# A pair-update kernel whose input is also laid out channel-major by the host, so that its first stage transposes no x

## The chip, the cores and the metric

One core of one Trainium2 chip runs the whole program. The metric is device time in microseconds (us) for one execution, lower is better; the kernel before is the median of three runs.

## The reference

x is 1 x 384 x 384 x 128 (i, j, channel), all float32. Two layers follow each other; cut to what is computed:

```python
# layer 0
z     = layernorm(x) * g + b
left  = (z @ Wl + bl) * sigmoid(z @ Wlg + blg)
right = (z @ Wr + br) * sigmoid(z @ Wrg + brg)
core  = einsum('bikh,bjkh->bijh', left, right)
zo    = (layernorm(core) * og + ob) @ Wout + bout
x1    = x + sigmoid(x @ Wg + bg) * zo
# layer 1
left  = x1 @ W_left + b_left + x1 @ W_eq + b_eq
right_sum = sum over j of (x1 @ W_right + b_right)
out   = (left * right_sum * sigmoid(x1 @ W_gate + b_gate)) @ W_out + b_out
y     = layernorm(out + x1) * scale + bias
```

## The kernel before

The program has three stages, one after the other; only their ends overlap.

**Stage 1** (source lines 100 to 403) makes `left` and `right`. A token is one (i, k) pair of x. The 384 x 384 tokens are cut into 144 chunks of 8 rows i by 128 tokens k, numbered so that 8 chunks (64 rows i of one block of 128 k) form a group; there are 18 groups. A chunk is two steps of 4 rows, so there are 288 steps and 16 steps in a group. `steps` (L352) lists them, and the loop at L368 writes out by hand what each engine is given in each step; `seq` keeps that order on every engine and DMA queue.

What happens to a step: `load_chunk` (L113) brings tokens on partitions and channels along the free axis. `stats` (L234) runs `bn_stats` and `bn_aggr` on VectorE (DVE), for the step that lies `AHEAD` = 6 steps further on. `powers` (L246), on GpSimd (POOL), makes for each token `rs` = 1/std and `nd` = mean - std, eight rows at a time, once per chunk. `shift` (L262), on GpSimd, subtracts `nd` from the 4 x 128 values of each token, two steps ahead. `front` (L272) transposes the four 128 x 128 blocks on TensorE (PE) and copies the result from PSUM on ScalarE (ACT), so that channels lie on partitions (`zt`). `back` (L319), called twice a step for two rows each, multiplies two blocks of `zt` by the folded 128 x 512 weights `wz`; ScalarE takes the sigmoid of the gate half with `rs` as its scale, and VectorE multiplies (L339) into a tile `lr` of one group (8 MiB, two buffers). The constant part of the layer norm is folded into `wz` with the matrix `avg` (`fold`, `weights`).

What stage 1 stores: `store_zt` (L299) writes each shifted and transposed step to the scratch tensor `xt_d`; `store_nd` (L301) transposes the `nd` of one group (64 rows) and writes it to `nd_d`; `store_slice` (L313) writes a finished group from `lr` to `lr_d`, one slice of 1 MiB per step, in the first eight steps of the next group. The last two groups stay in SBUF. All these DMAs are issued by SyncE (SP) in one order, and a DMA that waits holds up those behind it.

**Stage 2** (to L551) does, for each of 128 channels h, nine accumulating 128x128 by 128x384 matmuls (L516), and writes `core_d` and sums for the second layer norm. In its shade `early_x` (L484) rebuilds x for the first `TR` = 16 rows: it reads `nd` as a broadcast over partitions, adds `xt_d` by an accumulating DMA issued from GpSimd, and stores `xf_d`.

**Stage 3** runs over the 384 rows i: `front` (L633) makes the gate from x, `scale_core`, `layer0`, `gated_left`, `layer1`, the row layer norm, and `store`. Its x comes channel-major through `load_x` (a broadcast of `nd_d`, four rows at a time) and `add_x` (L588; an accumulating DMA from GpSimd that adds `xt_d`).

The four instructions of `powers`, which the prediction counts:

```python
seq(nc.gpsimd.tensor_scalar(sd, mv[:, :, 1], EPS, 1.0, ALU.add, ALU.mult))
seq(nc.gpsimd.tensor_tensor(rs, sd, mhalf[:, :hi - lo], ALU.pow))
seq(nc.gpsimd.tensor_tensor(sd, sd, rs, ALU.mult))
seq(nc.gpsimd.tensor_tensor(nd, mv[:, :, 0], sd, ALU.subtract))
```

Of the kernel before, what the change touches and what calls it, by code (L numbers as in the profile page):

```python
# [19 lines left out]
def triangle_then_gated_row_kernel(ctx: ExitStack, tc: tile.TileContext, a: dict, out: bass.AP):  # L20
# [14 lines left out]
    x = a["x"].rearrange("b i j c -> (b i) j c")  # L35
    y = out.rearrange("b i j c -> (b i) j c")
    N, _, C = x.shape
# [9 lines left out]
    TR = 16  # L47
# [6 lines left out]
    xt_d = dpool.tile([C, N, NB, P], F32, name="xt_d")  # L54
    nd_d = dpool.tile([N, N], F32, name="nd_d")
    xf_d = dpool.tile([C, TR, N], F32, name="xf_d")

# [24 lines left out]
    with ExitStack() as ctx2:  # L82
# [17 lines left out]
        with tc.tile_pool(name="p1w", bufs=6, side="right") as wp, \  # L100
             tc.tile_pool(name="p1x", bufs=6, side="right") as xp, \
             tc.tile_pool(name="p1s", bufs=5, side="right") as sp, \
             tc.tile_pool(name="p1z", bufs=6, side="right") as ztp, \
# [4 lines left out]
            AHEAD = NQ + 4  # L108
            HS = H // 8
            loaded, normed = {}, {}  # L110
            lr, full = {}, []

            def load_chunk(n, part=slice(0, XR)):  # L113
                if n < len(chunks):
                    kb, ig, c = chunks[n]
                    i0 = ig * G + c * XR
                    if part.start == 0:
                        loaded[n] = xp.tile([P, XR, C], F32, tag="xt", name="xt")
                    src = x[i0:i0 + XR, kb * P:(kb + 1) * P, :].rearrange("i k c -> k i c")
                    seq(nc.sync.dma_start(out=loaded[n][:, part], in_=src[:, part]))  # L120


            load_chunk(0, slice(0, 4))

            stage = lrp.tile([P, H, G, 2], F32, tag="lr", name="stage").rearrange("p h i s -> p (h i s)")

# [7 lines left out]
            seq(nc.vector.memset(avg, 1.0 / P))  # L136
# [21 lines left out]
            def fold():  # L158

                busy(2)
                busy(1, 1)
                seq(nc.gpsimd.tensor_tensor(d, b0, g0, ALU.subtract))
                seq(nc.gpsimd.tensor_tensor(m1, avg, d.to_broadcast([P, P]), ALU.mult))

                for p, gs in zip((p0, p1), halves):
                    seq(nc.tensor.matmul(p[:, gs], lhsT=m1, rhs=wst[:, gs], start=True, stop=False))
                    seq(nc.tensor.matmul(p[:, gs], lhsT=avg, rhs=brow[:, gs], start=False, stop=True))
# [35 lines left out]
            def late_weights():  # L205
# [3 lines left out]
                m2 = wp.tile([P, 4, C], F32, tag="z", name="m2", bufs=2)[:, 0]  # L209
                seq(nc.vector.tensor_scalar(m2, avg, go, -1.0, ALU.mult, ALU.mult))  # L210
# [23 lines left out]
            def stats(n, q, half):  # L234

                if q == 0 and half == 0:
                    normed[n] = [sp.tile(s, F32, tag=t, name=t) for t, s in
                                 (("st", [P, XR, 6]), ("mv", [P, XR, 2]), ("rs", [P, XR]), ("sd", [P, XR]))]
                st, mv, _, _ = normed[n]
# [3 lines left out]
                for r in range(r0, r0 + 2):  # L243
                    seq(nc.vector.bn_aggr(mv[:, r, :], st[:, r, :]))  # L244

            def powers(n, q):  # L246


                if n == 0 or q == NQ - 1:
                    lo, hi = (4 * q if n == 0 else 0), 4 * q + 4  # L250
                    _, mv, rs, sd = normed[n]
                    mv, rs, sd = mv[:, lo:hi], rs[:, lo:hi], sd[:, lo:hi]
                    kb, ig, c = chunks[n]
                    if c == 0 and lo == 0:
                        nds[kb, ig] = dp.tile([P, G], F32, tag="nd", name="nd")
                    nd = nds[kb, ig][:, c * XR + lo:c * XR + hi]
                    seq(nc.gpsimd.tensor_scalar(sd, mv[:, :, 1], EPS, 1.0, ALU.add, ALU.mult))  # L257
                    seq(nc.gpsimd.tensor_tensor(rs, sd, mhalf[:, :hi - lo], ALU.pow))
                    seq(nc.gpsimd.tensor_tensor(sd, sd, rs, ALU.mult))
                    seq(nc.gpsimd.tensor_tensor(nd, mv[:, :, 0], sd, ALU.subtract))  # L260

            def shift(n, q):  # L262

                kb, ig, c = chunks[n]
                z = wp.tile([P, 4, C], F32, tag="z", name="z", bufs=2)
                nd = nds[kb, ig][:, c * XR + 4 * q:c * XR + 4 * q + 4]
                seq(nc.gpsimd.tensor_tensor(  # L267
                    z, loaded[n][:, 4 * q:4 * q + 4, :], nd.unsqueeze(2).to_broadcast([P, 4, C]), ALU.subtract
                ))
                return z  # L270

            def front(n, q, z):  # L272

                pt = tps.tile([P, 4, P], F32, tag="pt", name="pt")
                for r in range(4):
                    seq(nc.tensor.transpose(pt[:, r, :], z[:, r, :], ident))  # L276
                zt = zts[n, q] = ztp.tile([P, 4, P], F32, tag="zt", name="zt")
                seq(nc.scalar.copy(zt, pt))

            def first_step():  # L280

                z = wp.tile([P, 4, C], F32, tag="z", name="z", bufs=2)
                zt = zts[0, 0] = ztp.tile([P, 4, P], F32, tag="zt", name="zt")
                nd = nds[chunks[0][:2]][:, 0:4]
                pts = [tps.tile([P, 4, P], F32, tag="pt", name="pt") for _ in range(2)]
                pairs = slice(0, 2), slice(2, 4)
                for s in pairs:
                    seq(nc.gpsimd.tensor_tensor(
                        z[:, s], loaded[0][:, s, :], nd[:, s].unsqueeze(2).to_broadcast([P, 2, C]), ALU.subtract
                    ))  # L290
                for s, pt in zip(pairs, pts):
                    for r in range(2):
                        seq(nc.tensor.transpose(pt[:, r, :], z[:, s.start + r, :], ident))
                    seq(nc.scalar.copy(zt[:, s], pt[:, 0:2]))

            def store_zt(n, q):
                kb, ig, c = chunks[n]
                i0 = ig * G + c * XR + 4 * q
                seq(nc.sync.dma_start(out=xt_d[:, i0:i0 + 4, kb, :], in_=zts.pop((n, q))))  # L299

            def store_nd(kb, ig):  # L301

                pt = tps.tile([P, 4, P], F32, tag="pt", name="pt")
                seq(nc.tensor.transpose(pt[:G, 0], nds.pop((kb, ig)), ident))
                ndt = dp.tile([G, P], F32, tag="ndt", name="ndt")
                seq(nc.scalar.copy(ndt, pt[:G, 0]))
                seq(nc.sync.dma_start(out=nd_d[ig * G:(ig + 1) * G, kb * P:(kb + 1) * P], in_=ndt))
# [11 lines left out]
            def back(n, q, half, between=None):  # L319
# [7 lines left out]
                for r in range(2):  # L327
                    seq(nc.tensor.matmul(  # L328
                        pr[:, r, :], lhsT=zts[n, q][:, 2 * half + r, :], rhs=wz, start=True, stop=True
# [4 lines left out]
                rs = [normed[n][2][:, r:r + 1] for r in range(r0, r0 + 2)]  # L334
# [18 lines left out]
            zs = {}  # L353
            nds, zts = {}, {}
            for k in range(AHEAD):
                for half in range(2):
                    stats(*steps[k], half)
# [8 lines left out]
                if k == 1:  # L366
                    zs[1] = shift(*steps[1])
            for k, (n, q) in enumerate(steps):  # L368
                if k + 2 < len(steps):
                    zs[k + 2] = shift(*steps[k + 2])  # L370
                if k + AHEAD - 1 < len(steps):
                    powers(*steps[k + AHEAD - 1])
                for half in range(2):
                    if k == 0:

                        back(n, q, half, (lambda: front(*steps[1], zs.pop(1))) if half else None)
                    else:
                        back(n, q, half)
                        if half == 0 and k + 1 < len(steps):
                            front(*steps[k + 1], zs.pop(k + 1))  # L380
                    if k + AHEAD < len(steps):
                        stats(*steps[k + AHEAD], half)
                if q == NQ - 1:
                    del loaded[n], normed[n]
                    load_chunk(n + 6)

                if chunks[n][2] == G // XR - 1 and q == (NQ - 1 if n < len(chunks) - 1 else NQ - 2):
                    store_nd(*chunks[n][:2])
                store_zt(n, q)
                if k == 0:  # L390
                    for i in range(4, 6):
                        load_chunk(i)
# [55 lines left out]
        with tc.tile_pool(name="p2r", bufs=2, side="right", reuse_waits="tile") as rrp, \  # L448
# [35 lines left out]
            def early_x(h):  # L484


                for n, step in enumerate((6, 8, 11)):
                    i, odd = divmod(h - step, 5)
                    if not odd and 0 <= i < TR:
                        if n == 0:  # L490
                            early[i] = rp.tile([P, N], F32, tag="ve", name="xe", bufs=NB)
                            seq(nc.sync.dma_start(out=early[i], in_=nd_d[i].partition_broadcast(P)))
                        elif n == 1:
                            seq(nc.gpsimd.dma_start(
                                out=early[i], in_=xt_d[:, i].rearrange("c b k -> c (b k)"), accum_op=ALU.add
                            ))
                        else:
                            seq(nc.sync.dma_start(out=xf_d[:, i], in_=early.pop(i)))

            early = {}  # L500
            fill(0)
            for h in range(H):
                fill(h + 1)
                early_x(h)
# [52 lines left out]
    with ExitStack() as ctx3:  # L557
# [20 lines left out]
        def load_x(i0):  # L578

            if i0 < N:  # L580
                xt = xts[i0] = xp.tile([P, RG, N], F32, tag="xt", name="xt")
                seq(nc.sync.dma_start(
                    out=xt.rearrange("p i j -> p (i j)"),
# [311 lines left out]
```

## Time and profile before

| what | value |
|---|---|
| median of three runs (lowest, highest) | 3282.27 us (3282.17, 3283.37) |
| span of the profiled execution | 3281.2 us (the view gives no time around it; the median lies 1.1 us above) |
| PE busy in the span | 3257.7 us, 99% |
| DVE / ACT / POOL busy | 2488.3 / 1929.3 / 2286.7 us |
| stage 1, stage 2, stage 3 (by PE's first matmul of each) | to 1128, to some 1866, to 3281 us |
| busy from 200 to 400 us, in stage 1 | PE 200.00, DVE 153.09, ACT 111.14, POOL 110.77 us |
| granted TensorE clock | 0.998 mean |

Columns: a group of instructions is one source line, engine, operation and tile; "busy" is its time in all, "mean" that of one instruction, and the idle time before it is put down to what ended it. A float32 matmul appears as two records, so 1152 products of L328 are 2304 records. Pipelined matmuls overlap in the records: their mean is longer than the pace at which they follow each other, which the chain of waits shows. The windows view gives, for a stretch of time, the busy time of every engine, the mean busy share of the 16 DMA engines (packets in flight overlap a little, so it can exceed 1) and the GB/s that they moved. MB and GB are powers of ten.

### The profile page before, as it was taken

Reading aid. Unit: us, or ns where it says so; the run is one execution under the profiler, and the core shown is the slowest. Engines: PE = TensorE matmul, PEld = TensorE weight load, DVE = VectorE, ACT = ScalarE, POOL = GpSimd, SP = SyncE. Lnnn points to the kernel's source line nnn. Section 1 sums busy time; section 2 is a strip of 40 time slices with the busy share of each in tenths; the row PEclk is TensorE's granted clock in tenths of the full one; section 3 lists DMA queues with packets and bytes.
Section 4 is the critical chain, followed back from the end, with each engine's and each line's share of the span. In section 5 each row is a group of like instructions: output and inputs, shape, how many; then the busy total and the mean of one; then the engine's idle time right before and its main releaser. Section 6 shows DMA issues by size and latency. Waiting matters only on the chain.

```text
span 3281.2 us, 48289 instructions
## 1 busy us (share of the span) xinstructions
PE 3257.7 (99%) x12412; PEld 1982.5 (60%) x12412; DVE 2488.3 (76%) x8015; ACT 1929.3 (59%) x4045; POOL 2286.7 (70%) x3315
## 2 busy tenths in 40 slices
PE   9999999999999999999999999999999999999998
PEld 4444444444444566666666566667777777777775
DVE  7777777777777655555555588888888888888888
ACT  5555555555555533333333467677777777777776
POOL 5555555555555456666666578888888888888997
PEclk9999999999999999999999999999999999999999
DMA  6998998998999499999999899999999999999994
GB/s 175 275 281 255 278 281 256 277 278 260 276 281 265 151 296 303 304 301 305 302 283 283 277 311 265 275 275 280 271 272 281 272 270 278 275 273 273 271 252 127
DMA packets 922773, 883.15 MB, mean 269 GB/s; under 512 B 25425, under 2 KB 836945, under 8 KB 922498
## 3 DMA queue, kind: packets, MB, share of 16 engines
q1 hardware_dynamic: 905648, 802.58, 77.7%
q0 software_dynamic: 15616, 75.70, 13.5%
q8 instruction: 102, 1.67, 0.2%
q10 hardware_dynamic: 1234, 1.77, 0.1%
q14 instruction: 173, 1.42, 0.1%
HBM read 514.92 MB, written 365.04 MB: 268 GB/s over the span
## 4 chain that ended last, share of the span: by engine, by line
PE 95%; POOL 3%; DVE 1%; ACT 1%; issue 0%; DMA 0%; POOLq 0%; DVEq 0%; ACTq 0%
PE pr L328 30%; PE pc L516 22%; PE py L698 7%; PE pr L669 7%; PE pl L687 7%; PE pg L686 7%; PE pg L638 7%; PE pt L276 4%; PE py L699 4%; POOL cs L660 1%; POOL rs L718 1%; POOL yt L768 1%; ACT py L733 0%; DMA core_d<-ct 0%; DVE st L713 0%
## 5 line engine op out<-in xcount | busy, mean ns | idle before, releaser
L328 PE MATMUL pr<-wz,zt 128*128 128x512 f32 x2304 | 1038.9, 593 | 0.0
L337 ACT ACTIVATE sg<-pr,rs 128x256 f32<-128x256 f32 x1152 | 482.8, 470 | 497.1 <-PE pr L328 363.5
L516 PE MATMUL pc<-rr,lrh 128*128 128x384 f32 x2304 | 743.3, 486 | 0.3 <-DVE lr L339 0.3
L339 DVE SCALAR_TENSOR_TENSOR lr<-pr,rs,sg 128x256 f32<-128x256 f32 x1152 | 505.0, 480 | 266.3 <-ACT sg L337 217.8
L328 PEld LDWEIGHTS pr<-wz,zt 128*128 128x128 f32 x2304 | 413.7, 190 | 410.2 <-issue 345.5
L516 PEld LDWEIGHTS pc<-rr,lrh 128*128 128x128 f32 x2304 | 452.0, 196 | 291.8 <-issue 1.1
L733 ACT ACTIVATE py<-py,nm,rs 128x128 f32<-128x128 f32 x1149 | 493.2, 430 | 197.8 <-POOL rs L722 116.6
L527 DVE TENSOR_TENSOR csum<-csum,ct 128x1152 f32<-128x1152 f32 x127 | 184.0, 1449 | 336.0 <-ACT ct L525 336.0
L698 PEld LDWEIGHTS py<-wo,u 128*128 128x128 f32 x2304 | 376.6, 191 | 97.5
L660 POOL TENSOR_TENSOR cs<-ct,rt 128x384 f32<-128x384 f32 x380 | 425.8, 1127 | 9.2 <-DMA rt<-rstd_d 3.7
L768 POOL TENSOR_TENSOR yt<-yt,lnb 128x384 f32<-128x384 f32 x380 | 423.6, 1116 | 2.4 <-DVE yt L762 2.4
L525 ACT COPY ct<-pc 128x1152 f32<-128x1152 f32 x127 | 142.2, 1120 | 445.2 <-PE pc L516 427.8
L698 PE MATMUL py<-wo,u 128*128 128x128 f32 x2304 | 402.0, 275 | 0.0
L267 POOL TENSOR_TENSOR z<-xt,nd 128x512 f32<-128x512 f32 x287 | 298.8, 1041 | 35.8 <-POOL z L267 30.6
L257 POOL TENSOR_SCALAR sd<-mv 128x8 f32<-128x8 f32 (+1 forms) x145 | 28.5, 197 | 422.8 <-DVE mv L244 422.4
L713 DVE BATCH_NORM_STATS2 st<-py 128x6 f32<-128x128 f32 x1152 | 265.9, 286 | 67.7 <-PE py L699 66.1
L699 PE MATMUL py<-ident,x1T 128*128 128x128 f32 x1152 | 314.0, 273 | 0.0
L638 PE MATMUL pg<-xt,mat_L_conv_Wg 128*128 128x384 f32 x768 | 310.7, 487 | 3.3 <-ACT ct L540 1.7
L669 PE MATMUL pr<-cs,wc 128*128 128x384 f32 x768 | 313.8, 490 | 0.1
L687 PE MATMUL pl<-x1T,mat_L_conv_W_left 128*128 128x384 f32 x768 | 310.9, 487 | 0.9 <-ACT gT L640 0.8
L686 PE MATMUL pg<-x1T,mat_L_conv_W_gate 128*128 128x384 f32 x768 | 310.7, 486 | 0.9 <-ACT g L689 0.9
L479 POOL COPY rr<-lrh 128x768 f32<-128x768 f32 x128 | 177.0, 1383 | 152.2 <-DMA lrh<-lr_d 151.9
(121 smaller groups left out, 4879.2 us busy)
## 6 DMA issues: line engine op xcount, KB each, us to landing
lr_d<-lr SPq DMA_DIRECT2D x128, 1024.0 KB, 7.1
lrh<-lr_d SPq DMA_DIRECT2D x128, 768.0 KB, 7.7
xt_d<-zt SPq DMA_DIRECT2D x288, 256.0 KB, 5.6
xt<-in_x_dram SPq DMA_DIRECT2D x143, 512.0 KB, 7.2
ct<-core_d SPq DMA_DIRECT2D x95, 768.0 KB, 6.3
rt<-rstd_d SPq DMA_DIRECT2D x95, 768.0 KB, 7.9
out_dram<-yt SPq DMA_DIRECT2D x94, 768.0 KB, 6.6
core_d<-ct SPq DMA_DIRECT2D x125, 576.0 KB, 8.8
```

The source lines that it names most:

```text
L328: seq(nc.tensor.matmul(pr[:, r, :], lhsT=zts[n, q][:, 2 * half + r, :], rhs=wz, start=True, stop=True))
L337: seq(nc.scalar.activation(sg[r], pr[:, r, 2 * H:], AF.Sigmoid, scale=rs[r]))
L339: seq(nc.vector.scalar_tensor_tensor(t[:, :, c * XR + r0 + r, :], pr[:, r, :2 * H].rearrange("k (h s) -> k h s", s=2), rs[r], sg[r].rearra ...
L516: seq(nc.tensor.matmul(banks[ib], lhsT=t[:, kb, ib * P:(ib + 1) * P, 0], rhs=rr[:, kb], start=(kb == 0), stop=(kb == NB - 1),))
L638: seq(nc.tensor.matmul(pg[:, :N], lhsT=wg0, rhs=r["xT"], start=True, stop=True))
L660: seq(nc.gpsimd.tensor_tensor(cs, ct[:, i % RG], rt[:, i % RG], ALU.mult))
L669: seq(nc.tensor.matmul(pr[:, :N], lhsT=wc, rhs=r["cs"], start=True, stop=True))
L686: seq(nc.tensor.matmul(pg2[:, :N], lhsT=wgate, rhs=r["x1T"], start=True, stop=True))
L687: seq(nc.tensor.matmul(pl[:, :N], lhsT=wleft, rhs=r["x1T"], start=True, stop=True))
L698: seq(nc.tensor.matmul(py[:, s], lhsT=r["u"][:, s], rhs=r["wo"], start=True, stop=False))
L733: seq(nc.scalar.activation(py[:, s], py[:, s], AF.Identity, bias=bias, scale=scale))
L768: seq(engine.tensor_tensor(yt, yt, lnbb, ALU.add))
```

## The change

The host hands over x three times: `x_nat` (as before, but each token's 8 rows of a chunk contiguous), `x_tok` (channels first, per chunk) and `x_row` (channels first, four rows i at a time, for stage 3). The output comes back in a layout of its own, which the host turns round.

From chunk 8 (`PLAIN`) on, stage 1 loads each chunk twice: `x_nat` for the statistics alone and `x_tok` for the product. `nd` is transposed and written to `nd_d` in batches of 1, 1, 2, 2 and then 4 chunks, and read back for every step as a broadcast over 128 partitions (`load_shift`, a tile `bc` of 128 x 512); GpSimd subtracts it in place. The first 8 chunks, one group, keep the transposes, and work in place in a buffer of `lr`. VectorE runs `bn_stats` only; GpSimd joins the two half-variances that it leaves (five more small instructions per chunk in the first group, four after). Statistics run up to `LEAD` = 18 steps ahead instead of 6. `xt_d`, `xf_d`, `early_x` and `add_x` are gone: stage 3 loads `x_row`.

```diff
-    TR = 16
+    PLAIN = 8
...
-            AHEAD = NQ + 4
+            AHEAD, LEAD = 6, 18
+            TURN, FETCH = 9, 6
...
+            for size in [1, 1, 2, 2] + [4] * len(chunks):
...
+            def load_columns(n):
+                if PLAIN <= n < len(chunks):
+                    columns[n] = xcp.tile([P, XR, P], F32, tag="xt", name="xc")
+                    src = x_tok[n // NG8, n % NG8]
+                    seq(nc.sync.dma_start(out=columns[n].rearrange("c i k -> c (i k)"), in_=src))
+
+            def load_shift(n, q):
+                t = shifts[n, q] = bcp.tile([P, 4 * P], F32, tag="bc", name="bc")
+                seq(nc.sync.dma_start(out=t, in_=nd_d[n, 4 * P * q:4 * P * (q + 1)].partition_broadcast(P)))
...
-            seq(nc.vector.memset(avg, 1.0 / P))
+            seq(nc.vector.memset(avg, 2.0 / P))
...
+                seq(nc.gpsimd.tensor_tensor(g0, g0, g0, ALU.add))
...
-                for r in range(r0, r0 + 2):
-                    seq(nc.vector.bn_aggr(mv[:, r, :], st[:, r, :]))
...
-                    seq(nc.gpsimd.tensor_scalar(sd, mv[:, :, 1], EPS, 1.0, ALU.add, ALU.mult))
+                    seq(nc.gpsimd.tensor_tensor(mv, st[:, :, 1:3], st[:, :, 4:6], ALU.add))
+                    seq(nc.gpsimd.tensor_tensor(dv, st[:, :, 1], st[:, :, 4], ALU.subtract))
+                    seq(nc.gpsimd.tensor_tensor(dv, dv, dv, ALU.mult))
+                    seq(nc.gpsimd.tensor_scalar(sd, mv[:, :, 1], 4.0 / C, 4.0 * EPS, ALU.mult, ALU.add))
+                    seq(nc.gpsimd.tensor_tensor(sd, sd, dv, ALU.add))
                     seq(nc.gpsimd.tensor_tensor(rs, sd, mhalf[:, :hi - lo], ALU.pow))
                     seq(nc.gpsimd.tensor_tensor(sd, sd, rs, ALU.mult))
                     seq(nc.gpsimd.tensor_tensor(nd, mv[:, :, 0], sd, ALU.subtract))
+                    if n < PLAIN:
+                        seq(nc.gpsimd.tensor_scalar(nd, nd, 0.5, 0.0, ALU.mult, ALU.add))
+
+            def shift(n, q, rows=slice(0, 4)):
+                s = slice(4 * q + rows.start, 4 * q + rows.stop)
+                if n < PLAIN:
+                    nd = nds[n, n + 1][:, s].unsqueeze(2).to_broadcast([P, rows.stop - rows.start, C])
+                    seq(nc.gpsimd.tensor_tensor(loaded[n][:, s], loaded[n][:, s], nd, ALU.subtract))
+                else:
+                    z = columns[n][:, s].rearrange("c i k -> c (i k)")
+                    seq(nc.gpsimd.tensor_tensor(z, z, shifts.pop((n, q)), ALU.subtract))
...
-            def store_zt(n, q):
...
             for k, (n, q) in enumerate(steps):
                 if k + 2 < len(steps):
-                    zs[k + 2] = shift(*steps[k + 2])
-                if k + AHEAD - 1 < len(steps):
-                    powers(*steps[k + AHEAD - 1])
+                    shift(*steps[k + 2])
+                while powered < len(chunks) and 2 * NQ * (powered + 1) <= given:
+                    powers(powered, NQ - 1)
+                    powered += 1
+                turned = [b for b in batches if NQ * b[0] - TURN == k]
...
-                    if k + AHEAD < len(steps):
-                        stats(*steps[k + AHEAD], half)
+                    stats_to(2 * (k + min(LEAD, AHEAD + k + 1)) + half + 1)
...
+                for b in turned:
+                    store_nd(b)
+                if q == NQ - 1:
+                    load_columns(n + 4)
+                for m, mq in steps[k + FETCH:k + FETCH + 1]:
+                    if m >= PLAIN:
+                        load_shift(m, mq)
+                for m in fetch.get(k, []):
+                    load_chunk(m)
                 store_slice()
...
-            def early_x(h):
...
+                seq(nc.sync.dma_start(out=xt.rearrange("p i j -> p (i j)"), in_=x_row[i0 // RG]))
-        def add_x(i0):
...
-                    out=y[i0:i1].rearrange("i (b p) c -> p i b c", p=P),
+                    out=out[i0 // RG].rearrange("p (i c) -> p i c", i=RG)[:, i0 % RG:i0 % RG + i1 - i0],
```

The buffers: `bc` has 4, `columns` (`x_tok`) 4, `x_nat` 5. A `bc` for step k + 6 is issued in step k, into the buffer that the shift of step k + 2 frees, and only after the batch's `nd` has landed in `nd_d`; `x_tok` of chunk n + 4 waits for the products of chunk n.

## The prediction

> **What bounds the kernel now.** I read the windows first, for which engine is full in which stage, then the chain of waits inside stage 1, then the groups by line for prices, then GpSimd's order of time, and last the DMA.
>
> ```profile
> 200.00:400.00 200.00, 200.00 (x622) 98.50 (x621) 153.09 (x619) 111.14 (x261) 110.77 (x155) 1.00 0.95 273
> 1128.00:1866.00 738.00, 737.98 (x2289) 449.05 (x2290) 401.51 (x256) 288.73 (x255) 454.63 (x780) 1.00 0.95 294
> 1905.00:3262.00 1357.00, 1353.35 (x6481) 953.21 (x6480) 1189.02 (x4198) 989.42 (x2281) 1186.71 (x1626) 1.00 0.93 267
> ```
>
> The columns are PE, PEld, DVE, ACT, POOL, granted clock, DMA share, GB/s. PE is full in all three stages, at clock 1.00. So an edit gains only where it takes matmuls away, and only until another engine or the DMA is full. Stages 2 and 3 lose no matmul here; stage 1 does. Its chain:
>
> ```profile
> 159.94 0.44 PE pt L276 x4
> 160.38 3.44 PE pr L328 x8
> 163.81 0.44 PE pt L276 x4
> 164.25 3.44 PE pr L328 x8
> ```
>
> A step is 3.44 us of products and 0.43 of transposes (164.25 - 160.38 = 3.87), back to back. A group of 16 steps takes 16 x 3.87 = 61.9 us.
>
> **What the change takes off PE.** 272 of the 288 steps (all but the first 8 chunks) lose four transposes: 272 x 0.43 = **-117 us**. The `nd` transposes go from 18 to 37 (batches of 1, 1, 2, 2 and 33 more); four transposes take 0.43, so 19 x 0.11 = **+2 us**. A group can then go in 55.0 + 0.2 = 55.3 us, if all else keeps up. ACT loses its 0.585 us copy per step (L278), DVE its `bn_aggr` (172.7 us in all, L244); both were at 56% and 77% and have room (the double pace of statistics at the start, too: 8 x 0.2 + 4 x 0.43 = 3.3 us of DVE in a step of 3.87). GpSimd and the DMA get more.
>
> **GpSimd.** Its order of time for one chunk now:
>
> ```profile
> 300.34 0.20 POOL L257 TENSOR_SCALAR sd<-mv 128x8 f32<-128x8 f32 x1 [3.02 <-DVE mv L244]
> 300.62 1.64 POOL L258 TENSOR_TENSOR rs<-sd,mhalf 128x8 f32<-128x8 f32 x1
> 302.33 0.20 POOL L259 TENSOR_TENSOR sd<-sd,rs 128x8 f32<-128x8 f32 x1
> 302.61 0.20 POOL L260 TENSOR_TENSOR nd<-mv,sd 128x8 f32<-128x8 f32 x1
> 302.77 1.04 POOL L267 TENSOR_TENSOR z<-xt,nd 128x512 f32<-128x512 f32 x1
> ```
>
> A small instruction costs 0.20 us and the next starts 0.28 after it, so four take 2.43 us (300.34 to 302.77). Four more make 2.43 + 4 x 0.28 = 3.55; in the first group five more make 3.83. The shift now reads two whole inputs where one was a repeated scalar. No row has that shape; the nearest is `cs` (L660, two whole inputs of 384, 0.99 at the least and 1.13 in the mean) and 128 x 768 on two inputs (L550, 1.82): the slope is (1.82 - 0.99)/384 = 2.2 ns an element, so 512 take 0.99 + 0.28 = 1.27 (an estimate); at least the old 1.04, at most 1.27 x 1.30/0.99 = 1.67 by the slowest `cs`. I take 1.27, since L267 itself never varied in this stage (1.038 to 1.047), while `cs` ran beside a fuller DVE. Then a chunk is 3.55 + 2 x 1.27 + some 0.3 of waits = 6.4 us against PE's 6.88: 93% full, a lead that grows by half a microsecond per chunk. Upper end: 3.55 + 3.34 + 0.3 = 7.2 per chunk, 3.6 a step, and GpSimd is the bound: 272 x 0.16 = 43 us lost.
>
> **The start is dearer.** In the first 13 iterations the statistics catch up from 6 steps ahead to 18, so GpSimd is given one chunk's powers in every iteration, not in every second, and the shift that PE waits for stands behind them in its order. Before, the shift of step 2 ends at 15.05 us (14.01 + 1.04) and PE starts its products at 15.76. Three sets of powers lie ahead of it, with five more instructions each: 15 x 0.28 + 0.28 for `g0` = 4.5, so it ends at 19.5. Then six iterations of 3.83 + 1.04 = 4.87 and six of 3.55 + 1.04 = 4.59 bring the shift of step 14 to 76.3; PE starts step 14 at 77, against 15.76 + 12 x 3.87 = 62.2 now: **+15 us**. Bounds: 0 if the small ones hid in each other, 18 with waits of 0.2 per iteration. After this GpSimd starts the second group with no lead.
>
> **DMA.** The stage moves more, in less time. Per group now: 8.39 MB of `lr`, 4.19 of x, 4.19 of `xt_d` = 16.8 MB in 61.9 us, 271 GB/s, which is the 273 of the first row. After: `lr` 8.39, `x_nat` 4.19, `x_tok` 4.19, broadcast of `nd` 4.19 = 20.97 MB; in 55.3 us that is 379 GB/s. What can it do?
>
> ```profile
> 132.00:134.00 2.00, 2.00 (x9) 1.10 (x8) 1.77 (x7) 1.24 (x3) 1.80 (x3) 1.00 0.00 0
> 76.00:128.00 52.00, 52.00 (x169) 26.25 (x168) 40.46 (x167) 28.50 (x67) 28.25 (x41) 1.00 1.05 303
> 338.00:342.00 4.00, 4.00 (x13) 1.91 (x12) 3.10 (x14) 2.15 (x5) 2.58 (x5) 1.00 1.15 347
> 1887.00:1897.00 10.00, 10.00 (x32) 5.89 (x31) 8.38 (x19) 3.82 (x7) 5.03 (x6) 1.00 1.00 386
> 2120.00:2122.00 2.00, 2.00 (x11) 1.34 (x10) 1.76 (x9) 1.51 (x4) 0.80 (x3) 1.00 1.10 425
> ```
>
> Now it is idle at the end of a group and saturated for 52 us of it, at 303 GB/s in packets that are all 512 B in the packet records; stores of `lr` alone reach 347; loads with long rows (stage 3) reach 386, shortly 425. The new loads have runs of 4 KB and 2 KB, so I price `lr` at 347 (24.2 us) and the rest, 12.58 MB, between 425 and 366 (29.6 to 34.4; 366 GB/s is what 1885 to 1895 shows): 53.8 to 58.6 us a group, all of it at 347: 60.4. The middle, 56.2, is above PE's 55.3 already. And the stream is uneven: in the eight steps with `lr` slices the DMA is given 3.0 + 2.0 = 5.0 us of work per 3.44 us step, so 12 us pile up, and the eight others drain 1.4 us each. `bc` for step k + 6 is issued in step k behind that pile; it can be some 10 us late (5.5 steps less shift, landing and a `powers` ahead of it) before PE stands. On SP, the broadcast of a batch's first step also waits until `nd`'s small store has gone through the pile, with an `lr` slice and the next x loads queued behind it; the same queue waited 131.5 us for that store's source before:
>
> ```profile
> SPq L307 <- ACT ndt L306: 131.5, 16, 8.6
> ```
>
> So I take 2.5 us of stalls in each of the 16 groups with `lr` slices, **+40 us**; ends 0 and 5.1 x 16 = 82.
>
> By the Trainium skill, "DMA: Bandwidth & Descriptors", Specifications, a core's share of HBM is about 358 GB/s. The rows at 386 and 425 are above it, so it is no hard ceiling here over 10 us; as a mean over a group it would make 20.97/358 = 58.6 us, a sum 13 us worse than mine.
>
> **What else moves.** `xt_d`'s stores (5.6 us to landing, 288 on SP) go, with SP's waits for the copies; SP's place in a step is now set by `x_tok`, which waits for PE. In stages 2 and 3, `early_x`, 108 accumulating DMAs on GpSimd (0.93 and 0.87 us each, L591 and L494) and the broadcast go; PE is full there, so 0, with at most 4 us from the places in 1905 to 3262 where PE is not busy (1357.0 - 1353.35). The output leaves in longer rows: only the last stores of 192 KB, 2.1 us each, could end sooner, under 1 us.
>
> **The sum.** -117 + 2 + 15 + 40 = -60: span 3281.2 - 60 = 3221; the median lies 1.1 above the span, so **3222 us**.
>
> **The rivals.**
> - *The DMA keeps pace.* For it: 53.8 us a group at the better rates, and 10 us of room for `bc`. Against: 379 GB/s is above all rows but two short ones. It gives -117 + 2 + 15 = -100, 3182 us. Chance 0.24.
> - *The DMA or GpSimd eats most of it.* Rates of 347 throughout (60.4 a group), or a shift of 1.67 us, which costs the same 43 us as half of that: 5.1 x 16 = 82 instead of 40, 3264 us; with the start at 18, 3267. For it: this core's long saturated stretches are at 303 to 347. Chance 0.16.
> - *Slower: the DMA is the bound of stage 1.* Place: groups 2 to 17, where `lr` slices, two x loads and the broadcast share 16 engines. Price: if the mix runs at the 303 GB/s of the saturated stretch, 20.97/303 = 69.2 us a group; 16 x (69.2 - 55.3) = 222, sum +122, 3404 us at worst. It decides from 55.3 + 100/16 = 61.6 us a group, 340 GB/s. Against: 303 was with 512 B throughout and with dips to 235 and 278 (392 to 396, 342 to 346 us) inside it, about once in the 10 us between two x loads, whose runs now get long. At a likelier 330 GB/s (63.5 us): 131 - 100, 3313 us. Chance 0.13.
>
> **How the numbers follow.** My forecast has 0.47. About 0.2% of the time, 6.5 us, is what a measurement of this kernel can tell from no change. Faster: forecast, first rival and nearly all of the second, 0.47 + 0.24 + 0.10 = 0.81; same: the rest of the second, 0.06; slower 0.13. The range leaves out the worst of the slower case and the small chance below the first rival: 3174 (no stalls, a start of 7) to 3278 (stalls of 5.8 in each of 16 groups, a start of 18).
>
> **What will show it.** L276 and L278 only in the first 62 us; a step of 3.44 us between stalls; the first 16 steps ending some 15 us late with PE waiting for the shift; PE idle inside stage 1 in the eight steps with `lr` slices, released by GpSimd, which waits for `bc`; the shift near 1.27 us; DMA share near 1 throughout. Wrong if the shift takes over 1.6 us, if DVE's statistics wait for `x_nat`, or if SP stands in front of `x_tok`, not of `bc`.

## The result, and the profile after

The changed kernel takes 3375.47 us (median of four runs, 3369.57 to 3378.28), the one before on the same chip 3282.65 (3282.17 to 3283.37): a ratio of 1.028, 95% interval 1.0266 to 1.0295. It is slower; the forecast was 3222.

The page of the kernel after, its span, its first part, the row of DMA shares (in tenths, 40 slices) and the first line of its chain:

```profile
span 3374.5 us, 45003 instructions
...
PE 3207.7 (95%) x11343; PEld 1892.4 (56%) x11343; DVE 2365.0 (70%) x6863; ACT 1817.1 (54%) x3792; POOL 2366.2 (70%) x3797
...
DMA  4999999999999859999999986566666666666653
...
PE 73%; DMA 3%; POOL 1%; issue 0%; ACT 0%; DVE 0%; SPq 0%; POOLq 0%; DVEq 0%; ACTq 0%
```

PE is busy 50 us less (3257.7 before), and yet the span is 93 us longer: PE waits. Stage 1 ends in slice 14; between its ends, in slices 1 to 12, the DMA is at 0.9 or more, and in stage 3 at 0.6. The windows of the same kernel, two of stage 1, one of stage 2 and one of stage 3 (columns as in the prediction: PE, PEld, DVE, ACT, POOL, granted clock, DMA share, GB/s):

```profile
200.00:400.00 200.00, 176.41 (x385) 75.78 (x386) 120.47 (x380) 80.89 (x196) 131.02 (x240) 0.93 0.97 309
400.00:600.00 200.00, 177.04 (x390) 75.50 (x389) 120.46 (x380) 81.79 (x198) 132.21 (x240) 0.95 0.99 314
1300.00:1900.00 600.00, 600.00 (x1862) 365.02 (x1861) 324.23 (x208) 236.31 (x207) 365.66 (x621) 1.00 0.92 283
2400.00:2800.00 400.00, 400.00 (x1908) 281.89 (x1907) 353.01 (x1231) 295.12 (x669) 322.26 (x447) 1.00 0.63 220
```

In stage 1 PE is full no more (200.00 before) and its clock is 0.93 to 0.95, no other engine is near full, and the DMA engines are at 0.97 to 0.99 while they move only 309 to 314 GB/s. Stages 2 and 3 are full of matmuls as before. Who releases PE is in its order of time over one group:

```profile
398.69 5.40 PE L348 MATMUL pr<-wz,xc 128*128 128x512 f32 x8 [2.31 <-POOL xc L296]
407.25 0.40 PE L322 MATMUL pt<-ident,nd 128*32 128x128 f32 x1 [3.16 <-POOL nd L283]
407.46 30.65 PE L348 MATMUL pr<-wz,xc 128*128 128x512 f32 x64
...
460.04 3.70 PE L348 MATMUL pr<-wz,xc 128*128 128x512 f32 x8 [1.22 <-POOL xc L296]
466.10 3.70 PE L348 MATMUL pr<-wz,xc 128*128 128x512 f32 x8 [2.35 <-POOL xc L296]
```

and GpSimd's order of time just before the wait of 3.16 us:

```profile
402.47 1.27 POOL L296 TENSOR_TENSOR xc<-xc,bc 128x512 f32<-128x512 f32 x1 [3.83 <-DMA bc<-nd_d]
403.69 0.22 POOL L276 TENSOR_TENSOR mv<-st 128x16 f32<-128x16 f32 x1
...
406.99 0.20 POOL L283 TENSOR_TENSOR nd<-mv,sd 128x8 f32<-128x8 f32 x1
```

GpSimd stands 3.83 us for a broadcast (`bc`). Behind the shift, in its order, lie the powers of another chunk; their last instruction (L283) makes the `nd` that PE is to transpose, and PE, in order too, stands 3.16 us for it with products behind it. The `lr` slices of this group are issued from 426.24 to 466.04 us: PE starves at the end of them, not all through them. Three windows, from just behind that wait to 456 us:

```profile
408.00:416.00 8.00, 8.00 (x13) 3.13 (x12) 2.24 (x7) 1.80 (x5) 6.48 (x11) 0.66 1.03 401
416.00:428.00 12.00, 12.00 (x29) 5.32 (x28) 8.77 (x29) 5.86 (x15) 8.03 (x18) 1.00 0.62 202
428.00:456.00 28.00, 28.00 (x67) 12.37 (x66) 20.69 (x67) 14.00 (x35) 19.79 (x34) 1.00 1.06 322
```

Once the slices are over, the DMA drains at 401 GB/s, stands idle for over a third of 12 us, and then is saturated at 322 GB/s. Work is thus lost at one end of a group and missed at the other.

**The sum, as measured.** I compare spans. From step 16 (the first product on the new operand) to the first matmul of stage 2 are 17 groups. Sixteen steps are 128 records of the products, so before, step 16 starts with the 129th record of L328, at 71.64 us, behind the transpose of `nd` (L304 at 71.53). Before, the 17 groups went from 71.6 to 1128.0 us, 1056.4; after from 84.4 to 1228.8, 1144.4. The last group has no slices to store and takes 55.5 us; the sixteen others take (1144.4 - 55.5)/16 = 68.1 each. The start cost 84.4 - 71.6 = 12.8. Stages 2 and 3 took 2145.7 instead of 2153.2.

### The profile page after: what moved, and what is told of

It is laid out like the page before. It is cut to its first block, busy times and chain, and to the rows that moved or that the text cites. A ratio compares the mean times of both kernels' runs of the same rounds, so it can differ in the third digit from the quotient of the medians.

```text
span 3374.5 us, 45003 instructions
## 1 busy us (share of the span) xinstructions
PE 3207.7 (95%) x11343; PEld 1892.4 (56%) x11343; DVE 2365.0 (70%) x6863; ACT 1817.1 (54%) x3792; POOL 2366.2 (70%) x3797
## 4 chain that ended last, share of the span: by engine, by line
PE 73%; DMA 3%; POOL 1%; issue 0%; ACT 0%; DVE 0%; SPq 0%; POOLq 0%; DVEq 0%; ACTq 0%
PE pc L538 22%; PE pr L348 11%; PE py L708 8%; PE pr L679 7%; PE pg L696 7%; PE pl L697 7%; PE pg L648 7%; PE py L709 4%; DMA bc<-nd_d 3%; POOL xc L296 0%; POOL rs L281 0%; DMA core_d<-ct 0%; PE pq L656 0%; ACT py L743 0%; PE pt L322 0%
## 5 line engine op out<-in xcount | busy, mean ns | idle before, releaser
L348 PE MATMUL pr<-wz,xc 128*128 128x512 f32 x2176 | 1000.3, 620 | 61.7 <-POOL xc L296 61.7
L348 PEld LDWEIGHTS pr<-wz,xc 128*128 128x128 f32 x2176 | 426.8, 199 | 616.9 <-issue 449.6
L296 POOL TENSOR_TENSOR xc<-xc,bc 128x512 f32<-128x512 f32 x272 | 342.3, 1270 | 278.2 <-DMA bc<-nd_d 170.3
L670 POOL TENSOR_TENSOR cs<-ct,rt 128x384 f32<-128x384 f32 x380 | 379.5, 1000 | 8.9 <-DMA rt<-rstd_d 7.7
L778 POOL TENSOR_TENSOR yt<-yt,lnb 128x384 f32<-128x384 f32 x380 | 380.3, 1002 | 2.9 <-DVE yt L772 2.8
L699 ACT ACTIVATE g<-pg,col_L_conv_b_gate 128x384 f32<-128x384 f32 x384 | 223.0, 581 | 103.0 <-PE pg L696 92.4
```

The costliest lines, as they stand in the source:

```text
L348: seq(nc.tensor.matmul(pr[:, r, :], lhsT=columns[n][:, 4 * q + 2 * half + r, :], rhs=wz, start=True, stop=True))
L778: seq(engine.tensor_tensor(yt, yt, lnbb, ALU.add))
```

## The experiments

Stage 1 below is always from step 16 to stage 2's first matmul. The theories: **bytes** (the DMA engines can't move the new mix fast enough), **pile** (eight slices in eight steps overload half of each group and leave the other half idle), **GpSimd's order** (in the expectations POOL ORDER: the powers behind a late broadcast hold up PE's transposes of `nd`).

### Spread the slices

```diff
-            HS = H // 8
+            sizes = [11] * 8 + [10] * 4
```

A group leaves `lr` in 12 slices, one a step. The lines that pass the sizes on are not shown.

> The finished group goes to lr_d in 12 slices, one per step, instead of 8; bytes and everything else as in the changed kernel (3375 us, 66 us per group in the profile). Theory BYTES (the mix of 20.97 MB per group runs at some 310 GB/s whatever its order): group stays at 65 to 67 us, total 3360 to 3385. Theory PILE (the eight steps with lr slices pile up work in front of the broadcast of the shift, and the DMA has room in the other eight): group falls to 58 to 61 us, total 3250 to 3300. Theory POOL ORDER (GpSimd waits in order, the nd transpose stands behind it): a little better, 3330 to 3370.

Measured 3285.83 us, beside 3283.3 for the kernel before. Its windows:

```profile
400.00:600.00 200.00, 187.52 (x423) 81.07 (x422) 130.55 (x412) 88.05 (x214) 144.35 (x266) 0.96 1.05 340
600.00:800.00 200.00, 184.33 (x418) 79.54 (x417) 129.97 (x411) 87.63 (x212) 140.37 (x254) 0.97 1.04 334
```

The pile cost 1144.4 - 1055.1 = 89 us of stage 1: the idle time of the DMA is gone, its share is above 1 throughout. But it now stops at (1055.1 - 55.5)/16 = 62.5 us in a group with slices, with 20.97 MB in it: 336 GB/s. PE is still not full.

### Take away the broadcasts

```diff
+                if (n, q) == (PLAIN, 0):
+                    only.append(bcp.tile([P, 4 * P], F32, tag="bc", name="bc"))
...
+                shifts[n, q] = only[0]
```

One broadcast is loaded and serves every shift.

> Leaves out the broadcast loads but for one, which every shift uses (wrong shift values); nd is still transposed and stored. 16.8 MB per group. BYTES: 54 us of DMA, so PE at 55.3 is the bound: 3375 - 16 x 10.7 = 3204 us. PILE and POOL ORDER: nothing waits for a broadcast any more, the same 3190 to 3210. If the shift or the powers on GpSimd were the bound, it would stay above 3300. It also prices the rest of the sum: -117 + 2 + 15 - 7 gives 3174 to 3185.

Measured 3169.68 us.

```profile
400.00:600.00 200.00, 200.00 (x473) 88.31 (x472) 147.14 (x465) 98.50 (x241) 159.31 (x291) 1.00 0.95 302
```

PE is full, the DMA is not, although the slices are still piled up. Stage 1 is 939.3 us, 55.3 a group: exactly what the prediction had for the matmuls alone. The transposes, those of `nd` included, are therefore worth 939.3 - 1056.4 = -117.1 us, and all that the DMA adds is 1144.4 - 939.3 = 205 us.

### Take away the natural loads

These are as many bytes as the broadcasts, and the broadcasts stay.

```diff
+                    elif n >= PLAIN + 5:
+                        loaded[n] = first5[n % 5]
+                        return
```

> Keeps the broadcasts and their order, leaves out the natural-layout loads after 13 chunks (statistics of old tokens are used). The same 4.19 MB per group less as without broadcasts, in long runs. BYTES: as without broadcasts, 3200 to 3215. PILE: less work in the pile (4.3 instead of 5.0 us per step), so 3220 to 3270. If broadcast reads are what is slow (their packets take 116 ns in the mean, 84 in the median), it gains much less than the run without broadcasts: 3280 to 3330.

Measured 3270.5 us.

```profile
400.00:600.00 200.00, 190.05 (x436) 83.18 (x435) 135.89 (x429) 91.42 (x223) 144.23 (x263) 0.97 0.91 281
```

```profile
POOL xc L301 <- DMA bc<-nd_d: 75.5, 44, 5.6
PE pt L327 <- POOL nd L288: 52.3, 13, 5.5
```

As many bytes as without broadcasts, and 101 us slower than that; the DMA is not full, and PE waits for `nd` 13 times (the waits view: us in all, times, longest). So with slices in a pile and the statistics 18 steps ahead, a broadcast is late even with 16.8 MB in a group. It does not follow that bytes are no cause: the pile and the short lead are still in this run, and no run has these bytes with only one of the two.

### Statistics two chunks earlier

```diff
-            AHEAD, LEAD = 6, 18
+            AHEAD, LEAD = 6, 22
```

with 16 buffers for `rs` instead of 14. First with slices in eight steps, then spread:

> Statistics run 22 steps ahead instead of 18, so the nd of a batch is ready two chunks earlier when PE comes to transpose it. POOL ORDER: PE's waits for nd (67 us from 195 to 1100 us) go: 3310 to 3340. BYTES and PILE: the wait only moves to the shift, 3365 to 3385.

> Even slices (12 per group) and statistics 22 steps ahead. With even slices the DMA moved 336 to 340 GB/s without a pause, 62 us a group, and PE still waited 54 us for nd and ran 38 us longer in its matmuls at a granted clock of 0.97. BYTES (20.97 MB at 338 GB/s): the group stays at 62 us, total 3275 to 3290. POOL ORDER (PE's waits for nd and the clock that they cost): group falls to 57 to 59 us, total 3205 to 3240.

Measured 3368.88 and 3284.82 us, 6.6 less than the change (whose own four runs lie 8.7 apart) and 1.0 less than the spread slices alone. As long as all the bytes are moved, GpSimd's order falls as a theory. Its wait is gone, and PE waits elsewhere. The waits of the second of these two, and its window:

```profile
POOL xc L296 <- DMA bc<-nd_d: 103.4, 74, 3.5
PE pr L348 <- POOL xc L296: 78.2, 84, 2.4
```

```profile
400.00:600.00 200.00, 183.61 (x421) 76.87 (x421) 129.95 (x410) 87.30 (x213) 143.75 (x263) 1.00 1.05 339
```

PE waits 78.2 us for the shift instead of 54.5 for `nd` (spread slices alone), in short pieces that leave the clock at 1.00. The DMA moves the same 339 GB/s. The colder clock and the wait for `nd` are both removed, and together they were worth 1055.1 - 1053.2 = 2 us of stage 1.

### Fewer bytes with the slices spread

The edits of the spread slices, of the earlier statistics and of the natural loads together.

> As the run with even slices and 22 steps, and leaves out the natural-layout loads after 13 chunks (statistics of old tokens). 16.8 MB per group, every broadcast kept. BYTES: 50 us of DMA at 338 GB/s, so PE at 55.3 is the bound: 3175 to 3200. If broadcasts are slow by themselves, or their chain of waits is (nd stored, landed, read back, subtracted): above 3225.

Measured 3172.76 us.

```profile
400.00:600.00 200.00, 200.00 (x473) 88.31 (x472) 147.26 (x466) 98.33 (x240) 159.12 (x290) 1.00 0.96 302
```

All 272 broadcasts are there, with their way through `nd_d`, and PE is full: stage 1 takes 941.9 us, 2.6 more than without broadcasts. So the way of `nd` through memory costs next to nothing by itself; it costs when 20.97 MB are moved, or with the pile and the short lead of the 3270.5 us above. Which of these two counted there stays open, since this run changes both.

### Why does the mix stop at 338 GB/s?

Both on the spread slices with the earlier statistics. The second operand of the shift is loaded from 128 different rows of `x_tok`, or from one row of `x_tok` repeated 128 times, in place of the broadcast of `nd`; neither waits for `nd` to land. Only the argument that changes is shown.

```diff
-    in_=nd_d[n, 4 * P * q:4 * P * (q + 1)].partition_broadcast(P)
+    in_=x_tok[n // NG8, n % NG8][:, 4 * P * q:4 * P * (q + 1)]
```

```diff
+    in_=x_tok[n // NG8, n % NG8][0, 4 * P * q:4 * P * (q + 1)].partition_broadcast(P)
```

> As the run with even slices and 22 steps, but the second operand of the shift is loaded from 128 different rows of x_tok instead of one row of nd repeated (wrong shift values; no wait for nd). The same bytes, packets and order. BYTES: the same as that run within 15 us. If repeated reads of one row are slow (mean packet 110 to 118 ns against a median of 84): 30 us or more faster than that run.

> As the run that loads 128 different rows of x_tok (3237 us), but one row of x_tok repeated 128 times, as nd is (wrong shift values; still no wait for nd). If the repeated reads of one row are what cost 48 us there: 3275 to 3290. If it was the wait for the stored nd: 3230 to 3245.

Measured 3237.0 with different rows and 3278.07 with one row, against 3284.82 for the real broadcast. The windows of the first and of the second:

```profile
200.00:400.00 200.00, 191.63 (x443) 81.48 (x443) 137.10 (x433) 92.33 (x225) 152.28 (x280) 1.00 1.07 360
400.00:600.00 200.00, 190.25 (x439) 80.94 (x438) 136.94 (x432) 91.35 (x222) 144.34 (x262) 1.00 1.06 350
600.00:800.00 200.00, 188.53 (x433) 79.12 (x431) 134.95 (x426) 89.81 (x219) 146.60 (x270) 1.00 1.06 353
```

```profile
400.00:600.00 200.00, 184.29 (x423) 77.29 (x422) 130.45 (x413) 87.46 (x213) 144.49 (x263) 1.00 1.05 340
600.00:800.00 200.00, 182.56 (x413) 76.16 (x412) 128.99 (x408) 86.09 (x210) 139.90 (x256) 0.99 1.04 335
```

The wait for `nd` to land is worth 1053.2 - 1046.8 = 6 us of stage 1, less than the 8.7 us by which the four runs of the change differ. Reading one row 128 times instead of 128 rows costs 1046.8 - 1005.9 = 41 us: the bytes are equal, the DMA is full both times, the rate is lower. Even so, at 350 to 360 GB/s, it is (1005.9 - 55.5)/16 = 59.4 us in a group with slices, and PE still waits. The last 1005.9 - 939.3 = 67 us are the bytes.

The packet records of the trace say which bytes are dear. In the run with spread slices and earlier statistics, from 150 to 1080 us, a packet of 512 B (`lr`) takes 27 ns on its engine, one of 2 KB (the broadcast) 115 and one of 4 KB (both loads of x) 174 in the mean. Worked out from these, as an estimate, 16 engines carry 303, 286 and 377 GB/s, and a group needs 27.7 + 14.7 + 22.3 = 64.7 us of packets; at a share of 1.04 that is 62 us, beside the (1053.2 - 55.5)/16 = 62.4 measured. So the short packets of `lr` are 40% of the bytes and 43% of the time. With 128 different rows the 2 KB packets take 98 ns.

### Fewer chunks in the new form

If bytes bind, a mix of old and new chunks should do better: an old one costs PE 0.87 us of transposes more and saves 524 KB of `x_tok` and as much of broadcast. Every second chunk from chunk 9 in the new form, then three of four; slices spread, `nd` stored in batches of 2 and of 3, and the buffers of x divided anew. Some lines of three of four:

```diff
-            batch = {n: b for b in batches for n in range(*b)}
+            turned_chunks = [n for n in range(PLAIN + 1, len(chunks)) if n % 4]
+            tok = {n: i for i, n in enumerate(turned_chunks)}
+            batches = [tuple(turned_chunks[i:i + 3]) for i in range(0, len(tok), 3)]
+            batch = {n: b for b in batches for n in b}
```

> Computes the reference. From chunk 9 on only every second chunk comes channel-major with a broadcast; the others keep the transposes, with statistics 6 steps ahead; even slices. 16.8 MB per group. PE per group 8 x 3.87 + 8 x 3.44 + 0.2 = 58.7 us. BYTES: 50 us of DMA, so PE is the bound: 3282 - 136 x 0.43 + 2 + 4 - 7 = 3223, faster than both kernels. If the broadcast's chain of waits stops PE anyway: 3250 to 3300.

> The kernel with every second chunk again, timed in rounds: 3227 within 5, a ratio of 0.983 to before.

> Computes the reference. From chunk 9 on three of four chunks come channel-major with a broadcast, one keeps the transposes; statistics 22 steps ahead, even slices. 18.9 MB per group; PE 12 x 3.44 + 4 x 3.87 + 0.3 = 57.1 us. BYTES at 338 GB/s: 55.8 us, just under PE, so 3200 to 3215, if the two do not get in each other's way; at 330 GB/s it is level. If the DMA needs more room than 2%: 3215 to 3240, no better than every second chunk (3227).

Every second chunk: 3226.9 in one run, and 3225.39 us in four (3224.78 to 3226.94), ratio 0.9827 (0.9812 to 0.9841). Three of four: 3205.18 us (3204.07 to 3206.61), ratio 0.9765 (0.9749 to 0.9781), faster than both kernels. Windows of the first and of the second:

```profile
400.00:600.00 200.00, 200.00 (x556) 93.78 (x555) 138.27 (x436) 105.65 (x253) 146.53 (x289) 1.00 0.95 290
```

```profile
400.00:600.00 200.00, 199.21 (x511) 90.31 (x510) 141.90 (x448) 100.99 (x244) 150.89 (x287) 1.00 1.04 332
600.00:800.00 200.00, 200.00 (x515) 91.03 (x514) 142.36 (x450) 102.00 (x247) 153.15 (x289) 1.00 1.04 335
```

With every second chunk the DMA has room; with three of four PE is just full while the DMA moves 332 to 335 GB/s at a share of 1.04. That is the balance: at all four of four the demand passes what the DMA gives.

## Why the prediction was wrong, point by point

| term | predicted, us | measured, us |
|---|---|---|
| transposes off PE, `nd` on it | -117 + 2 | -117.1 (stage 1 without broadcasts against before) |
| start | +15 | +12.8 |
| stalls for the DMA | **+40** (0 to 82) | **+205.1** |
| stages 2 and 3 | 0 (at most -4) | -7.5 |
| sum | -60 | +93.3 |

- **The step that failed** is the price of the DMA, "I take 2.5 us of stalls in each of the 16 groups", with its upper end of 82 in all. It was 205, 12.8 in each (68.1 us a group against 55.3). Two things in it were wrong, the rate and the pile.
- **The rate:** "I price `lr` at 347 (24.2 us) and the rest, 12.58 MB, between 425 and 366", from rows of 2 to 10 us, 56.2 us a group in the middle. No mix of this stage kept that up. Over 200 us it gave 306 to 314 GB/s as the change stands, 334 to 340 with the slices spread, 350 to 360 with different rows. The 347 stands beside a DMA share of 1.15, and SP issues a load of x in its 4 us (at 338.47), so it is not `lr` alone. By the packets above, `lr` takes about 27 of the 62.4 us, and the rest 36 (an estimate). The row that told it stood in the prediction, 303 GB/s over 52 us, and was set aside for its short packets, which `lr` keeps.
- **The pile** was foreseen ("12 us pile up"), but as a delay that the other eight steps make good. They don't: the DMA stood idle there for over a third of 12 us, and what it had not moved was then late.
- Taken away one after the other, the 205 are 89 of the pile, 2 of the earlier statistics, 6 of `nd`'s way through memory, 41 of rows read 128 times and 67 of bytes (89 + 2 + 6 + 41 + 67 = 205). This is one order, not prices that add up in any: with fewer bytes and spread slices, the broadcasts and `nd`'s way together cost only 941.9 - 939.3 = 2.6. The differences are between single executions, so the 2 and the 6 are not clear of noise.
- **The rival on the other side had the bound right**, and its point of decision, "61.6 us a group, 340 GB/s", holds: with the slices spread it is 62.5 us and 336 GB/s, and 3285.83 us beside 3283.3. At the 68.1 us of the change its sum makes 16 x (68.1 - 55.3) - 100 = +105; measured +93, since the start, the transposes and the later stages came out 12 us better. Its likelier 330 GB/s, 3313 us, lacked the pile, with which the change ran at 20.97/68.1 = 308. Its chance, 0.13, was too small.
- **The signs.** The shift is 1.27 us, as estimated from two rows; part of that is luck, since with the mean of `cs`, 1.13, in place of its least the same working gives 1.36. The powers take 3.5 us from 403.69 to 407.19 (predicted 3.55 with the gap after them). GpSimd is no bound: without broadcasts it is at 159.31 of 200 us. The wait for `bc` on GpSimd was named. That over half of PE's idle time comes through `nd` (77.8 us, and 61.7 for the shift) was not; with all the bytes moved it was of no account, since taking it away moved the wait to the shift. One sign of being wrong, SP standing in front of `x_tok` and not of `bc`, came half true: from 100 to 1150 us SP waited 281.0 us before `x_tok`, for PE to free its buffers, and 294 before `bc`.
- **The clock.** 77.8 + 61.7 = 139.5 us of waits in the stage are not 205; most of the other 66 are matmuls at a colder clock (the products are busy 1000.3 us, and 938.0 without broadcasts), which the prediction did not have. The run with spread slices and earlier statistics shows it as a symptom: at clock 1.00 the time is the same, since the DMA sets it.
- **Stages 2 and 3.** PE's part of stage 3 went from 1395.2 to 1390.8 us (with stage 2 equal, 743 us), and the tail behind the last matmul from 14.9 to 11.8. The first is about the limit of 4 us that was given, the second was priced under 1 us. No run takes these apart further.
- By the Trainium skill, "DMA: Bandwidth & Descriptors", Specifications, a core's share of HBM is about 358 GB/s. The 350 to 360 GB/s of the run with different rows lie at this figure over 200 us, the 401 GB/s over 8 us above lie over it, and no run shows that it is what binds here. As a mean it would have been nearer than the rates that I took, but not near: by the page's figure, an estimate, the stalls are 16 x (58.6 - 55.3) = 53 us.

**Open:** the 512-byte packets of `lr`, at 303 GB/s, are one reason why the mix with different rows ends at 350 to 360 GB/s where long-row loads showed 386 to 425 for short times. Why packets of 2 KB and 4 KB take 115 and 174 ns in the mean, with medians of 84 and 159, was not taken apart (stores beside loads, or the memory itself).

## What to carry to other kernels

Price a stage that fills the DMA by the longest saturated stretch of the trace with the same packets (52 us here), not by the best short one, and then ask how evenly the schedule feeds it, since a DMA that ran dry in one half of a cycle did not get the time back here (89 us). A change that trades matmuls for bytes need not be all or nothing: choose the share of chunks at which both engines are just full. And take no wait that ends last for the cause until it has been removed: here a wait and a colder clock were removed for 2 us, as another wait took their place.

## What was not expected of the hardware

- **Reading one row 128 times is slower than reading 128 rows.** 272 loads of 256 KB took stage 1 from 1005.9 to 1046.8 us, at the same bytes and DMA shares of 1.04 to 1.07 in both.
- **Short waits can cost the clock.** PE waits 2.31 us up to 398.69 and 3.16 us up to 407.25. The windows of the product's instructions alone (PE, PEld, clock, DMA share, GB/s), in the kernel after:

```profile
398.00:402.00 4.00, 3.31 (x5) 1.41 (x6) 0.72 1.11 329
408.00:412.00 4.00, 4.00 (x6) 1.47 (x5) 0.50 1.03 397
416.00:420.00 4.00, 4.00 (x11) 1.79 (x10) 1.00 0.56 197
```

  At 0.50 there are six records in 4 us instead of eleven. The Trainium skill, "TensorE: Matmul & The Clock Gate", Part 1, has the clock halve after an idle window of about 3.4 us. Here it fell after shorter waits: by the clock records of this trace it is at half from 399.74 to 403.15 and from 406.56 to 413.39. In the run with spread slices and earlier statistics waits of up to 2.2 us left it at 1.00, so the length of a wait alone does not decide it, and no run here shows what else does.
